# A Strassen-Winograd kernel on one core: two VectorE additions per half unit become one GpSimd addition, with a new GpSimd timetable

## The chip, the cores and the metric

The kernel runs on one core of a Trainium2 chip. The metric is the device time of one launch in microseconds; the median of three runs of the kernel before is 1453.6 us (1452.87 to 1454.05). The profile shown is one further execution of it, with a span of 1452.4 us on that core and a granted TensorE clock of 1.00.

## The reference

A factorization-machine layer over a batch of 1024 rows, 512 features and 64 embeddings of width 512, all in float32. Cut to what matters:

```python
out_lin = x @ lin_w.T + lin_b
xv = einsum('bf,efm->bem', x, weight)                  # x 1024x512, weight 64x512x512
zp = einsum('bf,efm->bem', square(x), square(weight))
return out_lin + 0.5 * sum(square(xv) - zp, axis=1)    # summed over the 64 embeddings
```

Because the second sum is linear in the squared weights, the kernel needs `square(weight)` summed over the embeddings only, and then one product with `square(x)`. The large part is `xv`: 64 products of 1024x512 by 512x512, each squared and added up.

## The kernel before, in words

**Groups and products.** Sixteen groups of four embeddings are worked through (`q` in the main loop, L542). In each, the product of x with the four weights is done by a two-level Strassen scheme in Winograd's form: seven outer products (named "1", "2", "6", "7", "5", "3", "4", in this order, `UNITS` L532), each of them seven inner products. A unit (`unit`, L413) is one outer product for one half `j` of 128 rows; it issues seven TensorE products `p`, each a 128x128 by 128x512 float32 matmul that the trace records as two matmuls, into the PSUM banks x, v and y.

**The timetable.** Every operation is registered with `st.at(t, fn)`, and `Stream.run` (L23) emits them in the order of t. A t orders the instructions in each engine's queue and nothing else: at run time each engine takes its queue in order and waits on semaphores. One group has 98 steps of t, fourteen per outer product, and the 98 products of a group fall on one step each, so a step is the time of one product p. Within a unit that begins at t0 the products stand at t0, +2, +4, ... +12, and the two halves j are seven steps apart and interleave. Work on bank contents is put half a step after the product it follows.

**Engines.** TensorE does the products. ScalarE copies bank x to bank y (L481), squares finished blocks in place (`squares`, L499) and squares weights (`w_squares`, L517). VectorE adds PSUM banks to blocks in SBUF: `to_s`, `join`, `out_of` (L440, L464, L450). GpSimd makes the weight combinations: `outer_t` (L373, 128x1024, two per combined outer operand) and `inner_t` (L384: tp of 128x1024, then t6 and t4 of 128x512, for each outer product). tp is read by TensorE from step 2 of its outer product on, t6 from step 4, t4 from step 12. The tiles tp, t6 and t4 have two buffers each. GpSimd also issues the DMAs that add to memory: `gather` (L509) adds squared blocks to `acc[0]` or `acc[1]` (128x1024, 512 KB each), `w_squares` adds squared weights to `w2_sum` (1 MB each). A gather into a part of `acc` waits for the one before it into the same part to have landed. SyncE loads the weights (`load_w`, L356, four of 1 MB in a group).

**Blocks.** Each group has three result tiles of [2 (u), 2 (j), 2, 512] per partition: "a", "b" and "c" (`place`, L407). "a" and "c" swap places from group to group. Outer product "5" is special (`both`, L417): its four results go to "a" and to "c" both. For the two results that come straight from a bank, `out_of` makes two VectorE additions from PSUM. For the other two, b = 3 and b = 1, `join` leaves the result in the SBUF tile `s`, and from there `rest_a` (L471, VectorE, 128x512, twice per j) adds it into "a" and `rest_dst` (L475, GpSimd, 128x1024, once per j) writes "b" plus it to "c". The next outer product, "3", reads "a" again in `to_s`.

**The end.** After the last group (`g = 98 * NQ`, L612) come `square(x)`, the combinations of it and of `w2_sum` on GpSimd (`last_sx`, `last_tw`), and one more seven-product Winograd step (`last_p`) in two halves s, whose results are joined with `acc`. The last squares of "a" are paired by GpSimd (`pair_up`, L745) and gathered, those of "b" are added to `acc[1]` by VectorE (`add_c21`, L749).

Of the kernel before, what the change touches and what calls it, by code (L numbers as in the profile page):

```python
# [10 lines left out]
ALU = mybir.AluOpType  # L11
# [17 lines left out]
def kernel(  # L29
# [383 lines left out]
    def unit(t0, q, i, j, addend, dst):  # L413


        d = {}
        both = i == "5"  # L417

        def p(o, bank, start):
            def fn():  # L420
                nc.tensor.matmul(  # L421
                    d[bank],
                    xsl(i, o)[:, ts(j, P)],
                    operand_b(q, i, o),
                    start=start,
                    stop=True,
                    skip_group_check=True,
                )

            return fn  # L430

        def p1():
            for n in "xvy":
                d[n] = psum.tile(
                    [P, BK], F32, tag=n, name=f"{n}{q}_{i}{j}", bufs=2 if n == "x" else 3
                )
            d["s"] = spool.tile([P, 2, BK], F32, tag="s", name=f"s{q}_{i}{j}")
            p("1", "x", True)()

        def to_s(bank, b):  # L440
            def fn():
                o = d["s"][:, b // 2]
                if addend is None or both:
                    nc.scalar.copy(o, d[bank])
                else:
                    nc.vector.tensor_add(o, d[bank], zblk(q, addend, j, b))  # L446

            return fn

        def out_of(bank, b):  # L450
            def fn():
                if addend is None:
                    nc.scalar.copy(zblk(q, dst, j, b), d[bank])
                    return
                if both:
                    z = zblk(q, "a", j, b)
                    nc.vector.tensor_add(z, d[bank], z)  # L457
                nc.vector.tensor_add(  # L458
                    zblk(q, dst, j, b), d[bank], zblk(q, addend, j, b)
                )  # L460

            return fn

        def join(bank, b):  # L464
            def fn():
                s = d["s"][:, b // 2]
                nc.vector.tensor_add(s if both else zblk(q, dst, j, b), d[bank], s)  # L467

            return fn

        def rest_a(b):  # L471
            z = zblk(q, "a", j, b)
            nc.vector.tensor_add(z, z, d["s"][:, b // 2])  # L473

        def rest_dst():  # L475
            nc.gpsimd.tensor_add(
                place(q, dst)[:, 1, j], place(q, addend)[:, 1, j], d["s"]
            )

        st.at(t0 + 0, p1)  # L480
        st.at(t0 + 0.5, lambda: nc.scalar.copy(d["y"], d["x"]))  # L481
        st.at(t0 + 2, p("5", "v", True))
        st.at(t0 + 2.5, to_s("v", 3))
        st.at(t0 + 4, p("6", "y", False))
        st.at(t0 + 4.5, to_s("y", 1))
        st.at(t0 + 6, p("2", "x", False))
        st.at(t0 + 6.5, out_of("x", 0))
        st.at(t0 + 8, p("7", "y", False))
        st.at(t0 + 8.5, join("y", 3))
        st.at(t0 + 10, p("3", "v", False))  # L490
        st.at(t0 + 10.5, join("v", 1))
        st.at(t0 + 12, p("4", "y", False))
        st.at(t0 + 12.5, out_of("y", 2))
        if both:
            st.at(t0 + 9.6, lambda: rest_a(3))
            st.at(t0 + 11.6, lambda: rest_a(1))
            st.at(t0 + 12.6, rest_dst)

    def squares(t, q, n, j, wait):  # L499
        z = place(q, n)  # L500
# [6 lines left out]


    def gather(t, q, n, r, j, u):  # L509
        st.at(  # L510
            t,
            lambda: nc.gpsimd.dma_start(  # L512
                acc[r][:, j], place(q, n)[:, u, j], accum_op=ALU.add
            ),
        )

    def w_squares(t, q, v, u):  # L517
        first = q == v == u == 0

        def sq(kk):  # L520
            o = (w2_sum if first else w2_sb)[:, ts(kk, 2)]
            nc.scalar.activation(o, WB[kk][v][:, u], AF.Square)  # L522

        for kk in range(2):
            st.at(t + 0.1 * kk, lambda kk=kk: sq(kk))
        if not first:
            st.at(
                t + 3.5,
                lambda: nc.gpsimd.dma_start(w2_sum, w2_sb, accum_op=ALU.add),
            )  # L530

# [10 lines left out]
    for q in range(NQ):  # L542
        g0 = 98 * q
        last = q == NQ - 1
        for kk, v, t in ((1, 0, -41), (0, 1, -39), (0, 0, -37), (1, 1, -10)):
            if q:
                st.at(g0 + t, lambda q=q, kk=kk, v=v: load_w(q, kk, v))

        for i, t0, t1 in (
            ("5", -13.4, -10.2) if q else ("5", -11, -10.9),  # L550
            ("6", 11, 14.1) if q else ("6", 0.5, 0.6),
            ("7", 24, 24.1),
            ("4", 50, 50.1),
        ):
            for u, t in enumerate((t0, t1)):
                st.at(g0 + t, lambda i=i, u=u: outer_t(i, u))
        for i, *times in (
            ("1", -6.4, -2.9, -2.8) if q else ("1", -11.5, -11.4, -11.3),
            ("2", 3.1, 7.1, 7.2) if q else ("2", -5, -4.9, -4.8),
            ("6", 18.4, 22.1, 22.2),  # L560
            ("7", 31.1, 31.2, 38.1),
            ("5", 43.1, 43.2, 49.1),
            ("3", 57.9, 58, 61.6),
            ("4", 73.1, 80.1, 80.2),
        ):
            for n, t in zip(("tp", "t6", "t4"), times):
                st.at(g0 + t, lambda q=q, i=i, n=n: inner_t(q, i, n))
        for n, (i, (addend, dst)) in enumerate(UNITS.items()):
            for j in range(2):
                unit(g0 + 14 * n + 7 * j, q, i, j, addend, dst)  # L570

        for k, n, r, times in (
            (1, "c", 0, (31, 43, 38, 49)),
            (4, "c", 1, (73, 84.5, 80, 91.5)),
            (5, "a", 0, (87.6, 99, 95, 105)),
            (6, "b", 1, (101, 112, 108.5, 120)),
        ):
            for j in range(2):
                t = g0 + 14 * k + 7 * j + 14.6
                squares(t - (0.95 if last and n == "b" else 0), q, n, j, 3 * (k == 4))  # L580
                if last and n != "c":
                    continue
                for u in range(2):
                    gather(g0 + times[2 * j + u], q, n, r, j, u)
        if q == 0:
            w_times = (-6, 14.8, 36, 54)
        else:
            w_times = (-15, 14.8, 36, 54)
        for n, t in enumerate(w_times):
            w_squares(g0 + t, q, n // 2, n % 2)  # L590
    for kk, v in ((0, 0), (1, 0), (0, 1), (1, 1)):
# [18 lines left out]


    g = 98 * NQ  # L612
    XQ = [WB[0][r].rearrange("p u l (n q) -> p u (l n) q", q=Q) for r in range(2)]
    SX, TW = {}, {}

    def load_xq(r):
# [9 lines left out]
        return SX[i]  # L626

    def last_sx(i):
        t = WB[1][0] if i in "56" else T5
        t = t.rearrange("p u l (n q) -> p u (l n) q", q=Q)  # L630
        SX[i] = t[:, "5673".index(i) % 2]
        a21, a22 = XQ[1][:, 0], XQ[1][:, 1]
# [10 lines left out]
        return w2_sum[:, ts(kk, 2), ts(u, HM)]  # L643

    def last_tw(i):
        t = WB[1][1].rearrange("p u l m -> p (u l m)").rearrange(
            "p (n l c) -> p n l c", l=2, c=HM
        )
        TW[i] = t[:, "5674".index(i)]
# [28 lines left out]
    def last_banks(s):  # L678
        for n in "xvy":
            L[n, s] = psum.tile(  # L680
                [P, BK], F32, tag=n, name=f"{n}_last{s}", bufs=2 if n == "x" else 3
            )

        L["o", s] = place(NQ - 1, "c")[:, s]
        L["t", s] = w2_sb.rearrange("p (r u) c -> p r u c", r=2)

    def blk(n, s, b):
        return L[n, s][:, b // 2, b % 2]
# [52 lines left out]
        )  # L741

    def pair_up(j):  # L745
        z = place(NQ - 1, "a")
        nc.gpsimd.tensor_add(z[:, 0, j], z[:, 0, j], z[:, 1, j])

    def add_c21(j, u):  # L749
        o = acc[1][:, j]  # L750
        nc.vector.tensor_add(o, o, ZT[1][:, u, j])  # L751

    for j in range(2):
        st.at(g - 10.5 + 7 * j, lambda j=j: pair_up(j))
        gather(g - 7.7 + 7 * j, NQ - 1, "a", 0, j, 0)
        for u in range(2):
            st.at(g + (4.6 + 0.1 * u, 8.65)[j], lambda j=j, u=u: add_c21(j, u))

    for r, t in ((1, -39), (0, -37)):
        st.at(g + t, lambda r=r: load_xq(r))  # L760
    for t, r, kk in ((-26, 1, 0), (-25, 1, 1), (-22, 0, 0), (-21, 0, 1)):
        st.at(g + t, lambda r=r, kk=kk: square_xq(r, kk))
    for i, t in zip("5673", (-18, -15, -12, -2)):
        st.at(g + t, lambda i=i: last_sx(i))
    for i, t in zip("5674", (-9, -8, -6, -5)):
        st.at(g + t, lambda i=i: last_tw(i))
    for s, ks in ((0, (0, 3.2, 5.2, 6, 7, 8, 9)), (1, (10, 12, 14, 16, 18, 20, 22))):
        k1, k5, k6, k2, k7, k3, k4 = (g + k for k in ks)
# [19 lines left out]
        else:  # L788
# [5 lines left out]
            for j in range(2):  # L794
                st.at(k4 + j, lambda j=j: end_p(j))
                st.at(k4 + j + 0.5, lambda j=j: end_out(j))
                st.at(k4 + j + 0.6, lambda j=j: store(1, 2, slice(j, j + 1)))
    for t, b in ((11.1, 0), (12.1, 2)):
        st.at(g + t, lambda b=b: last_t(1, b))
    for t, b in ((11.1, 0), (11.2, 1), (11.3, 2), (11.4, 3)):  # L800
        st.at(g + t, lambda b=b: add_acc(0, b))
# [36 lines left out]
```

## Time and profile before

| what | value | where from |
|---|---|---|
| median of three runs | 1453.6 us | the times |
| span of the profiled run | 1452.4 us | the page |
| ScalarE busy | 621.8 us (43%) | the page, part 1 |
| 128x1024 additions on GpSimd, tp from a combined operand, mean as recorded | 3021 ns | groups of instructions, L391 |
| `rest_a` on VectorE | 64 of 1950 ns | groups, L473 |
| `rest_dst` on GpSimd | 32 of 2606 ns | groups, L476 |
| gathers, issue to landing, median | 250 of 7.2 us | DMA issues |
| additions to w2_sum, issue to landing, median | 63 of 9.2 us | DMA issues |
| weight loads, issue to landing, median | 64 of 11.9 us | DMA issues |
| share of the 16 DMA engines, 741 to 828 us | 0.89, at 194 GB/s | busy time by stretch |

How to read it. PE is TensorE's matmuls, DVE VectorE, ACT ScalarE, POOL GpSimd. In a line of the groups, `z<-z,s` names the tile written and the tiles read, and the tail gives the idle time of the engine just before those instructions and what ended it. A line of the waits gives the engine and line that waited, who ended the wait, the sum of the waits in us, how many there were and the longest. Starts and durations in a timeline are us from the span's start. A GpSimd instruction that follows the start of a DMA is recorded from its own dispatch[...]; so costs of GpSimd are read from one end to the next, not from the durations.

### The profile page before, as it was taken

The numbers are of one execution on the slowest core, as the hardware profiler recorded it, in microseconds if no ns is written. First come the engines' busy times: TensorE is split into PE (matmuls) and PEld (weight loads), VectorE is DVE, ScalarE is ACT, GpSimd is POOL, SyncE is SP. The second block draws the span as 40 slices with busy tenths as digits, with TensorE's granted clock in tenths as the row PEclk, the third lists the DMA queues.
The fourth block names the chain that finished last, engine by engine and source line by source line (L and its number), as shares of the span: only waits on it lengthen the run. The fifth ranks groups of instructions, "written<-read, shape, count | busy, mean of one in ns | idle before, by whom it ended". The sixth has DMA issues, their size and how long they took to land.

```text
span 1452.4 us, 11321 instructions
## 1 busy us (share of the span) xinstructions
PE 1411.4 (97%) x3340; PEld 631.5 (43%) x3340; DVE 993.4 (68%) x1341; ACT 621.8 (43%) x824; POOL 1241.6 (85%) x836
## 2 busy tenths in 40 slices
PE   9999999999999999999999999999999999999998
PEld 5444444444444444444444444444444444444446
DVE  6785767857577585766857567585766858567687
ACT  3344353452534444353453534444353453435343
POOL 7778979888897988979888897988979888897984
PEclk9999999999999999999999999999999999999999
DMA  5389898898988889898898988889898898988864
GB/s 210 65 201 213 179 204 173 209 188 204 199 170 212 172 203 210 187 197 169 211 186 202 202 170 212 176 200 212 196 190 165 213 178 206 206 170 212 176 147 115
DMA packets 66749, 272.59 MB, mean 188 GB/s; under 512 B 6400, under 2 KB 8960, under 8 KB 58368
## 3 DMA queue, kind: packets, MB, share of 16 engines
q0 software_dynamic: 45072, 197.15, 69.1%
q1 hardware_dynamic: 21328, 74.19, 16.3%
q10 hardware_dynamic: 288, 0.52, 0.1%
q8 instruction: 27, 0.44, 0.1%
q14 instruction: 34, 0.28, 0.1%
HBM read 72.61 MB, written 2.10 MB: 51 GB/s over the span
## 4 chain that ended last, share of the span: by engine, by line
PE 81%; DVE 9%; issue 5%; POOL 4%; DMA 1%; ACT 0%; DVEq 0%; POOLq 0%
PE y L421 34%; PE x L421 23%; PE v L421 22%; DVE z L473 3%; DVE s L446 1%; PE lin L216 1%; POOL t L393 1%; POOL t L380 1%; DMA acc<-z 1%; DVE s L467 1%; DVE z L458 1%; DVE z L457 1%; DVE z L467 1%; POOL acc L512 1%; DVE acc L751 1%
## 5 line engine op out<-in xcount | busy, mean ns | idle before, releaser
L421 PE MATMUL y<-t,xs 128*128 128x512 f32 x896 | 425.9, 594 | 20.1 <-DVE z L467 19.5
L512 POOL DMA_DIRECT2D acc<-z x250 | 287.8, 1170 | 130.1 <-ACT z L504 70.2
L481 ACT COPY y<-x 128x512 f32<-128x512 f32 x224 | 127.8, 571 | 516.2 <-PE x L421 516.2
L467 DVE TENSOR_TENSOR z<-y,s 128x512 f32<-128x512 f32 x192 | 132.5, 690 | 226.7 <-PE y L421 226.7
L504 ACT ACTIVATE z<-z 128x1024 f32<-128x1024 f32 x256 | 256.8, 1053 | 68.6 <-DVE z L458 68.6
L421 PEld LDWEIGHTS y<-t,xs 128*128 128x128 f32 x896 | 168.2, 190 | 241.5 <-issue 227.6
L421 PE MATMUL x<-w,xs 128*128 128x512 f32 x512 | 248.4, 592 | 0.0
L421 PE MATMUL y<-tp,xs 128*128 128x512 f32 x448 | 230.4, 596 | 15.0 <-DVE s L446 15.0
L421 PE MATMUL v<-tp,xs 128*128 128x512 f32 x448 | 229.0, 593 | 0.0
L391 POOL TENSOR_TENSOR tp<-w 128x1024 f32<-128x1024 f32 x64 | 194.2, 3034 | 0.0
L421 PE MATMUL x<-t,xs 128*128 128x512 f32 x384 | 188.3, 592 | 0.0
L467 DVE TENSOR_TENSOR z<-v,s 128x512 f32<-128x512 f32 x192 | 132.4, 690 | 68.4 <-PE v L421 66.6
L380 POOL TENSOR_TENSOR t<-w,t 128x1024 f32<-128x1024 f32 x64 | 168.3, 2712 | 0.0
L458 DVE TENSOR_TENSOR z<-y,z 128x512 f32<-128x512 f32 x192 | 132.0, 688 | 51.3 <-PE y L421 51.1
L458 DVE TENSOR_TENSOR z<-x,z 128x512 f32<-128x512 f32 x192 | 131.8, 687 | 33.3 <-PE x L421 31.8
L522 ACT ACTIVATE w_sb<-w 128x1024 f32<-128x1024 f32 x126 | 125.8, 1047 | 63.5 <-DMA w_sum<-w_sb 63.5
L421 PEld LDWEIGHTS x<-w,xs 128*128 128x128 f32 x512 | 97.3, 190 | 122.0 <-issue 121.7
L391 POOL TENSOR_TENSOR tp<-t 128x1024 f32<-128x1024 f32 x48 | 145.0, 3021 | 0.0
L421 PEld LDWEIGHTS y<-tp,xs 128*128 128x128 f32 x448 | 83.8, 190 | 127.4 <-issue 98.8
L421 PEld LDWEIGHTS v<-tp,xs 128*128 128x128 f32 x448 | 84.9, 190 | 107.8 <-issue 104.3
L421 PE MATMUL v<-w,xs 128*128 128x512 f32 x256 | 130.7, 592 | 0.0
L446 DVE TENSOR_TENSOR s<-v,z 128x512 f32<-128x512 f32 x160 | 110.3, 689 | 23.8 <-PE v L421 23.3
(115 smaller groups left out, 1569.9 us busy)
## 6 DMA issues: line engine op xcount, KB each, us to landing
acc<-z POOLq DMA_DIRECT2D x250, 512.0 KB, 7.2
w<-weight SPq DMA_DIRECT2D x64, 1024.0 KB, 11.9
w_sum<-w_sb POOLq DMA_DIRECT2D x63, 1024.0 KB, 9.2
w<-x SPq DMA_DIRECT2D x2, 1024.0 KB, 10.1
out<-z SPq DMA_DIRECT2D x7, 256.0 KB, 2.2
xs<-x SPq DMA_DIRECT2D x2, 384.0 KB, 6.8
t<-lin_wT ACTq DMA_DIRECT2D x2, 256.0 KB, 4.3
t<-lin_wT SPq DMA_DIRECT2D x1, 512.0 KB, 6.3
```

The source lines that it names most:

```text
L216: nc.tensor.matmul(LIN[n], quarter(0, kk, (0, 1, 3, 2)[2 * s + l])[:, ts(j, P)], lw_sb[:, 2 * kk + l, :], start=(kk == 0 and l == 0), stop ...
L380: nc.gpsimd.tensor_sub(OUTER[i][:, u], a[:, u], b[:, u])
L391: nc.gpsimd.tensor_sub(t, b[:, 1], b[:, :, 0])
L421: nc.tensor.matmul(d[bank], xsl(i, o)[:, ts(j, P)], operand_b(q, i, o), start=start, stop=True, skip_group_check=True,)
L446: nc.vector.tensor_add(o, d[bank], zblk(q, addend, j, b))
L458: nc.vector.tensor_add(zblk(q, dst, j, b), d[bank], zblk(q, addend, j, b))
L467: nc.vector.tensor_add(s if both else zblk(q, dst, j, b), d[bank], s)
L473: nc.vector.tensor_add(z, z, d["s"][:, b // 2])
L481: st.at(t0 + 0.5, lambda: nc.scalar.copy(d["y"], d["x"]))
L504: lambda u=u: nc.scalar.activation(z[:, u, j], z[:, u, j], AF.Square),
L512: lambda: nc.gpsimd.dma_start(acc[r][:, j], place(q, n)[:, u, j], accum_op=ALU.add),
L522: nc.scalar.activation(o, WB[kk][v][:, u], AF.Square)
```

## The change

For outer product "5", the two `rest_a` additions of VectorE for each j (128x512 each) become one GpSimd addition of 128x1024, next to the one that `rest_dst` makes; VectorE then keeps only additions that read a PSUM bank in the main loop. GpSimd gets this work in place of DMA starts: the gathers of the first "c" and of "b" take both halves j in one DMA of 1 MB instead of two of 512 KB. All t of GpSimd's operations in a group are set anew, and with them those of the weight squares. At the end of the kernel, the pairing of the last "a" squares on GpSimd is dropped: four of the last eight blocks of squares are gathered and four are added by VectorE at later places, the loads of x go to other buffers, and the first combination of the squared x is put between the additions of the last outer product "5".

```diff
-        def rest_a(b):
-            z = zblk(q, "a", j, b)
-            nc.vector.tensor_add(z, z, d["s"][:, b // 2])
-        def rest_dst():
-            nc.gpsimd.tensor_add(
-                place(q, dst)[:, 1, j], place(q, addend)[:, 1, j], d["s"]
-            )
+        def rest(n, src):
+            nc.gpsimd.tensor_add(place(q, n)[:, 1, j], place(q, src)[:, 1, j], d["s"])
...
-            st.at(t0 + 9.6, lambda: rest_a(3))
-            st.at(t0 + 11.6, lambda: rest_a(1))
-            st.at(t0 + 12.6, rest_dst)
+            st.at(t0 + 11, lambda: rest("a", "a"))
+            st.at(t0 + 13.8, lambda: rest(dst, addend))
...
-                t + 3.5,
+                t + 5,
                 lambda: nc.gpsimd.dma_start(w2_sum, w2_sb, accum_op=ALU.add),
...
-            ("5", -13.4, -10.2) if q else ("5", -11, -10.9),
-            ("6", 11, 14.1) if q else ("6", 0.5, 0.6),
-            ("7", 24, 24.1),
-            ("4", 50, 50.1),
+            ("5", -8, 2) if q else ("5", -11, -10.9),
+            ("6", 14.2, 14.3) if q else ("6", 0.5, 0.6),
+            ("7", 28.7, 28.8),
+            ("4", 50, 53),
...
-            ("1", -6.4, -2.9, -2.8) if q else ("1", -11.5, -11.4, -11.3),
-            ("2", 3.1, 7.1, 7.2) if q else ("2", -5, -4.9, -4.8),
-            ("6", 18.4, 22.1, 22.2),
-            ("7", 31.1, 31.2, 38.1),
-            ("5", 43.1, 43.2, 49.1),
-            ("3", 57.9, 58, 61.6),
-            ("4", 73.1, 80.1, 80.2),
+            ("1", -4.3, -0.6, 2.1) if q else ("1", -11.5, -11.4, -11.3),
+            ("2", 6.4, 10.1, 10.2) if q else ("2", -5, -4.9, -4.8),
+            ("6", 20.7, 20.8, 27),
+            ("7", 34.4, 34.5, 39.7),
+            ("5", 43.1, 43.2, 43.3),
+            ("3", 57.9, 58, 61.7),
+            ("4", 81, 81.1, 81.2),
...
-            (1, "c", 0, (31, 43, 38, 49)),
-            (4, "c", 1, (73, 84.5, 80, 91.5)),
-            (5, "a", 0, (87.6, 99, 95, 105)),
-            (6, "b", 1, (101, 112, 108.5, 120)),
+            (1, "c", 0, ((None, 38.8), (None, 52.9))),
+            (4, "c", 1, ((0, 73), (0, 87), (1, 80), (1, 92.8))),
+            (5, "a", 0, ((0, 88), (0, 99.5), (1, 96.5), (1, 107.2))),
+            (6, "b", 1, ((None, 111.3), (None, 124.2))),
...
-    for j in range(2):
-        st.at(g - 10.5 + 7 * j, lambda j=j: pair_up(j))
-        gather(g - 7.7 + 7 * j, NQ - 1, "a", 0, j, 0)
-        for u in range(2):
-            st.at(g + (4.6 + 0.1 * u, 8.65)[j], lambda j=j, u=u: add_c21(j, u))
+    gather(g - 10, NQ - 1, "a", 0, 0, 0)
+    gather(g - 1.5, NQ - 1, "a", 0, 1, 0)
+    gather(g + 1.5, NQ - 1, "a", 0, 0, 1)
+    gather(g + 3.5, NQ - 1, "b", 1, 0, 0)
+    for t, n, r, j, u in (
+        (8.65, "b", 1, 1, 0),
+        (8.7, "b", 1, 1, 1),
+        (8.8, "a", 0, 1, 1),
+        (11.25, "b", 1, 0, 1),
+    ):
+        st.at(g + t, lambda n=n, r=r, j=j, u=u: add_last(n, r, j, u))
...
-    for i, t in zip("5673", (-18, -15, -12, -2)):
+    for i, t in zip("5673", (-24.1, -9.9, -9, -5)):
         st.at(g + t, lambda i=i: last_sx(i))
```

More of the change, by code (lines that the diff above doesn't have):

```diff
@@ L509, in gather, with fn @@
     def gather(t, q, n, r, j, u):
[L510 to L515, printed above, removed]
+        def fn():
+            z = place(q, n)[:, u]
+            o, z = (acc[r], z) if j is None else (acc[r][:, j], z[:, j])
+            nc.gpsimd.dma_start(o, z, accum_op=ALU.add)
+        st.at(t, fn)
     def w_squares(t, q, v, u):
@@ L579 @@
                 t = g0 + 14 * k + 7 * j + 14.6
-                squares(t - (0.95 if last and n == "b" else 0), q, n, j, 3 * (k == 4))
-                if last and n != "c":
-                    continue
-                for u in range(2):
-                    gather(g0 + times[2 * j + u], q, n, r, j, u)
+                squares(t - (0.95 if last and n == "b" else 0), q, n, j, 4 * (k == 4))
+            for m, (j, t) in enumerate(times):
+                if not last or n == "c":
+                    gather(g0 + t, q, n, r, j, m % 2)
         if q == 0:
-            w_times = (-6, 14.8, 36, 54)
+            w_times = (-6, 14.8, 37, 56.6)
         else:
-            w_times = (-15, 14.8, 36, 54)
+            w_times = (-15, 14.8, 37, 56.6)
         for n, t in enumerate(w_times):
@@ L612 @@
     g = 98 * NQ
-    XQ = [WB[0][r].rearrange("p u l (n q) -> p u (l n) q", q=Q) for r in range(2)]
+    XQ = [
+        t.rearrange("p u l (n q) -> p u (l n) q", q=Q) for t in (WB[0][1], WB[1][0])
+    ]
     SX, TW = {}, {}
@@ L628, in last_sx @@
     def last_sx(i):
-        t = WB[1][0] if i in "56" else T5
+        t = WB[0][0] if i in "56" else T5
         t = t.rearrange("p u l (n q) -> p u (l n) q", q=Q)
@@ L645, in last_tw @@
     def last_tw(i):
-        t = WB[1][1].rearrange("p u l m -> p (u l m)").rearrange(
+        t = w2_sb.rearrange("p k m -> p (k m)").rearrange(
             "p (n l c) -> p n l c", l=2, c=HM
@@ L684, in last_banks @@
         L["o", s] = place(NQ - 1, "c")[:, s]
-        L["t", s] = w2_sb.rearrange("p (r u) c -> p r u c", r=2)
+        L["t", s] = T6
     def blk(n, s, b):
@@ L741, in end_out, with add_last @@
         )
[L745 to L751, printed above, removed]
-    for j in range(2):
-        st.at(g - 10.5 + 7 * j, lambda j=j: pair_up(j))
-        gather(g - 7.7 + 7 * j, NQ - 1, "a", 0, j, 0)
-        for u in range(2):
-            st.at(g + (4.6 + 0.1 * u, 8.65)[j], lambda j=j, u=u: add_c21(j, u))
-    for r, t in ((1, -39), (0, -37)):
+    def add_last(n, r, j, u):
+        o = acc[r][:, j]
+        nc.vector.tensor_add(o, o, place(NQ - 1, n)[:, u, j])
+    gather(g - 10, NQ - 1, "a", 0, 0, 0)
[9 more added lines that the diff above has]
+        st.at(g + t, lambda n=n, r=r, j=j, u=u: add_last(n, r, j, u))
+    for r, t in ((1, -40.9), (0, -38.9)):
         st.at(g + t, lambda r=r: load_xq(r))
-    for t, r, kk in ((-26, 1, 0), (-25, 1, 1), (-22, 0, 0), (-21, 0, 1)):
+    for t, r, kk in ((-28, 1, 0), (-27.9, 1, 1), (-25, 0, 0), (-24.9, 0, 1)):
         st.at(g + t, lambda r=r, kk=kk: square_xq(r, kk))
-    for i, t in zip("5673", (-18, -15, -12, -2)):
+    for i, t in zip("5673", (-24.1, -9.9, -9, -5)):
         st.at(g + t, lambda i=i: last_sx(i))
-    for i, t in zip("5674", (-9, -8, -6, -5)):
+    for i, t in zip("5674", (-9.8, -9.7, -8.9, -4.9)):
         st.at(g + t, lambda i=i: last_tw(i))
@@ L797 @@
                 st.at(k4 + j + 0.6, lambda j=j: store(1, 2, slice(j, j + 1)))
-    for t, b in ((11.1, 0), (12.1, 2)):
+    for t, b in ((11.1, 0), (12.6, 2)):
         st.at(g + t, lambda b=b: last_t(1, b))
```

## The prediction, made before the changed kernel was run

> **What bounds the kernel now.** I read part 1 of the page first.
>
> ```profile
> PE 1411.4 (97%) x3340; PEld 631.5 (43%) x3340; DVE 993.4 (68%) x1341; ACT 621.8 (43%) x824; POOL 1241.6 (85%) x836
> ```
>
> TensorE is busy 97% of the span, so all that a change of order can win is its idle 41 us, and in the pipeline's refill after each idle stretch. Next, the waits: who kept TensorE waiting.
>
> ```profile
> PE y L421 <- DVE z L467: 19.5, 17, 1.2
> ...
> PE y L421 <- DVE s L446: 15.0, 16, 1.0
> ...
> PEld y L421 <- POOL t L393: 8.5, 17, 1.0
> ...
> PE y_last L666 <- DVE z L705: 1.6, 1, 1.6
> ```
>
> Two waits for VectorE, 16 times each: once per group. The timeline around one of them:
>
> ```profile
> 702.27 3.33 DVE L473 TENSOR_TENSOR z<-z,s 128x512 f32<-128x512 f32 x1
> ...
> 702.39 2.65 POOL L391 TENSOR_TENSOR tp<-t 128x1024 f32<-128x1024 f32 x1
> ...
> 705.52 0.68 DVE L467 TENSOR_TENSOR s<-v,s 128x512 f32<-128x512 f32 x1
> ...
> 706.12 0.68 DVE L446 TENSOR_TENSOR s<-y,z 128x512 f32<-128x512 f32 x1
> 706.28 2.35 POOL L476 TENSOR_TENSOR z<-z,s 128x1024 f32<-128x1024 f32 x1 [1.24 <-DVE s L467]
> 706.72 2.45 DVE L473 TENSOR_TENSOR z<-z,s 128x512 f32<-128x512 f32 x1
> ...
> 706.85 1.12 PE L421 MATMUL y<-tp,xs 128*128 128x512 f32 x2 [0.94 <-DVE s L446]
> ...
> 711.72 1.10 PE L421 MATMUL y<-t,xs 128*128 128x512 f32 x2 [1.16 <-DVE z L467]
> ```
>
> `rest_a` (L473) takes 3.33 and 2.45 us where GpSimd adds at the same time. VectorE's queue behind it comes late, and TensorE waits for `to_s` (L446) and then for a `join` (L467). The chain of waits shows these additions on the path, and a period:
>
> ```profile
> 706.80 2.10 DVE z L473
> ...
> 793.52 2.10 DVE z L473
> ```
>
> Period 86.72 us. An undisturbed product p takes 0.858 us (four matmul records are 1.72 us in the same chain), so 98 take 84.1: 2.6 us per group are lost. The matmul starts agree: after the four matmuls at the two waits the steps exceed 0.429 us by 1.10, 0.10, 1.33 and 0.07, together 2.60.
>
> GpSimd has the time left. Its costs, from one end to the next:
>
> ```profile
> 753.77 4.68 POOL L380 TENSOR_TENSOR w<-w,w 128x1024 f32<-128x1024 f32 x2
> 758.38 0.87 POOL L512 DMA_DIRECT2D acc<-z  x1
> 758.99 2.66 POOL L391 TENSOR_TENSOR tp<-w 128x1024 f32<-128x1024 f32 x1
> 761.73 1.27 POOL L393 TENSOR_TENSOR t<-w,tp 128x512 f32<-128x512 f32 x1
> 762.94 0.87 POOL L512 DMA_DIRECT2D acc<-z  x1
> 763.55 1.57 POOL L395 TENSOR_TENSOR t<-w,t 128x512 f32<-128x512 f32 x1
> ```
>
> The ends are 758.45, 759.25, 761.65, 763.00, 763.81, 765.12. So a 128x1024 addition costs 2.36 us (4.68 for two, 2.40 for the third), a 128x512 one 1.33, a DMA start 0.81; starts of 1 MB additions to w2_sum show the same 0.83.
>
> **What the Trainium skill says.** "SBUF — State Buffer", section "Who interferes with whom": a VectorE operation with two SBUF inputs shares a read interface with a GpSimd operation that reads SBUF, exclusively, and one fully blocks the other; with one SBUF input it doesn't. The trace agrees: L473 takes 0.69 to 3.33 us, additions with a PSUM input 0.67 to 0.69 whatever GpSimd does. "GPSIMD Engine Reference", section 3.1: a float32 `tensor_tensor` of 2048 elements takes 4497 ns on GpSimd; half of it is an estimate of 2.25 us for 1024, and the trace's 2.36 is what I use. "DMA: Bandwidth & Descriptors", section "Anatomy of one DMA": a DMA's semaphore wait is made by the issuing sequencer, so a gather that waits holds up all of GpSimd's queue; the trace has such waits of up to 3.8 us ("POOL acc L512 <- DMA acc<-z"). The same page, "Queues, rings and completion order": the DMA engines alternate between queues, so weight loads and additions share them; the trace shows landings of 4.6 us alone and 11 to 14 us in the crowded stretch.
>
> **The change part by part.**
>
> *VectorE.* 64 operations of 1950 ns leave its queue, 125 us. None of what remains in the main loop, but for eight short bias additions, has two SBUF inputs. In the tightest eight steps (6.9 us) around "5" and "3", eleven PSUM additions remain; back to back they take 0.60 each, 6.6 us, and each is released at least two steps before TensorE needs it. Both waits go: 16 x 2.6 = 41.7 us.
>
> *GpSimd's sum.* Before, per group: 17 additions of 128x1024, 14 of 128x512, 20 DMA starts: 17 x 2.36 + 14 x 1.33 + 20 x 0.82 = 75.1 us of 86.7. After: 19, 14 and 16: 44.8 + 18.6 + 13.1 = 76.6 of 84.1. 7.5 us are left for its waits.
>
> *GpSimd's timetable*, in steps (additions 2.75 and 1.55, DMA starts 0.95), where it must wait or is awaited:
> - The join before `rest("a")` of j = 0 ends about step 68.1. 70.9 `rest("a")`, 73.6 `rest("c")`, 74.6 gather. j = 1 is released at 75.1: 77.9, 80.6, gather 81.6. `to_s` of "3" reads "a" at 73 and 80: two steps (1.8 us) to spare each.
> - Queued behind are the operands of "4": tp 84.4 (due 86), t6 85.9 (due 88), t4 87.5 (due 96). 1.6 steps, 1.4 us, to spare; the narrowest place.
> - Then gathers and the next group: 88.4, 89.4, w2_sum 90.4, outer "5" 93.1, gather 94.1, tp "1" 96.8 (due 100), gather 97.8, t6 99.3 (due 102), gather 100.3, outer "5" 103, t4 104.6 (due 110), tp "2" 107.3 (due 114). The next gather waits for the one at 97.8 to land. Ahead of it are 3 MiB of additions and most of a 1 MB load from 87.5 on. In the trace 4 MiB took from step 86 to 111.2, 0.16 MiB a step; so it lands at about 111 to 112. Then t6 "2" ends at 114.5 (due 116), t4 116, gather 117, outer "6" 122.5, w2_sum 123.5, tp "6" 126.2 (due 128).
> - From there the queue gains: outer "7" ends at 136 (due 140), tp "7" 138.6 (due 142), tp "5" 146.3 (due 156), the fourth outer operand at 154 to 156, tp "3" 158.7 (due 170), t4 162.8. `rest("a")` is released at 166.1: 3.3 steps of rest. The period of 98 steps closes.
>
> *Five groups* have extra waits of TensorE for t6 or tp (periods of 87.1 to 87.4 in the chain): 2.4 us in all. The due times above leave 1.5 steps where these had none; I take them as gone, too.
>
> *DMA.* The merged gathers move the same bytes. In the trace's packet records a 4 KB addition packet takes 337 ns, an 8 KB one 639, so 35 ns are saved per pair. Per group the engines need 8 x 2.70 + 8 x 5.11 + 4 x 3.36 = 75.9 us of 84.1: share 0.90 as now. It costs nothing. "c" is overwritten at step 71 and its second gather, issued at 54 to 55, lands by 67 with the 9.2 us that 1 MB additions take.
>
> *The weight squares* move 2.6 steps later at 56.6; ScalarE then waits less for w2_sum (63.5 us in the waits now), off the path.
>
> *The end.* Two `add_c21` additions (9.5 us, blocked by GpSimd) stand ahead of the `minus_half` that TensorE waits 1.63 us for; after, they stand behind it: 1.9 us gone with the refill. They lie behind GpSimd's last work, where the trace shows 1.25 us each, so they end before the second half needs `acc`. Against this, in the last group a 128x1024 combination is put between the two j of `rest`: `rest("a")` of j = 1 ends at 80.1, tp of "4" at 86.5 instead of 86: 0.7 us lost.
>
> Sum: 41.7 + 2.4 + 1.9 - 0.7 = 45.3; 1453.6 - 45.3 = 1408.3. For GpSimd lateness of the kind that five groups show, I leave 0.7: 1409.
>
> **The rivals.**
> - *GpSimd takes VectorE's place as the one awaited*, at tp "4" or after the crowded gathers. For it: 1.4 us to spare, landings that vary by 2 us (11.2 to 14.1). Against: all other places have more, and eleven groups in sixteen lost nothing to GpSimd before. With 1 us per group: 1409 + 16 = 1425.
> - *VectorE still late.* Eleven additions in eight steps leave 0.3 us. If half the loss stays: 1409 + 21 = 1430.
> - *GpSimd becomes the bound.* If its waits of now (10.4 us in one group: 4.3 for squares, 3.6 for landings, 2.5 for VectorE) stay and the shorter period adds 1 us to the landings, the period is 76.6 + 10.4 + 1 = 88.0 against 86.9 on average now: 1453.6 + 16 x 1.1 - 1.2 = 1470, slower. Without the extra, no change. Against it: the waits now come partly from `rest_a` itself (3.1 us for a square behind it), and waits that lie inside the slack shrink by themselves.
>
> **How the numbers follow.** Forecast 0.73; GpSimd awaited 0.15; VectorE late 0.05; GpSimd the bound 0.05; no change 0.02. Low end: all waits gone and none new is 1453.6 - 46.0 = 1407.6; I take 1405 for unsure starts. High end: the first rival, 1426. That leaves out about 0.12. Faster 0.93, same 0.02, slower 0.05.
>
> **What would show it.** Right: waits of TensorE for `to_s` and `join` near zero; periods of 84.1 us; GpSimd's rows of `rest` near 2.36 us; GpSimd idle before `rest("a")`; DMA share about 0.90. Wrong: TensorE waiting for tp or t6 of "4", "2" or "6" in each group, or GpSimd's idle time before gathers above 7.5 us per group.

## The result, and the profile after

The changed kernel takes 1413.39 us (median of four runs, 1413.10 to 1414.48) against 1453.57 us before: a ratio of 0.9725, interval 0.9708 to 0.9742, or 40.2 us less. 1409 had been forecast, with 1405 to 1426 as the range. The profiled execution has a span of 1411.2 us, 41.2 less than the one before.

Part 1 of the page of the changed kernel:

```profile
PE 1402.8 (99%) x3340; PEld 633.7 (45%) x3340; DVE 883.1 (63%) x1277; ACT 623.2 (44%) x824; POOL 1244.5 (88%) x806
```

VectorE's busy time fell by 110 us. GpSimd's stayed where it was (1241.6 before), because 60 DMA starts paid for 32 more additions; of the shorter span it is 88% instead of 85%. TensorE is busy 99%.

The waits of the changed kernel, with who waited, for whom, the sum in us, the number and the longest:

```profile
POOL z L472 <- DVE s L467: 46.3, 31, 3.0
...
POOL acc L506 <- DMA acc<-z: 33.2, 20, 4.4
...
ACT w_sb L515 <- DMA w<-weight: 23.5, 12, 3.3
...
PEld y L421 <- POOL t L393: 4.8, 8, 1.3
...
PEld y L421 <- DVE s L446: 4.0, 4, 1.0
...
DVE acc L348 <- DMA acc<-z: 3.1, 4, 1.5
...
PE y L421 <- DVE z L467: 1.8, 1, 1.8
```

The 34.5 us in which TensorE waited for `to_s` (L446) and `join` (L467) are gone: of the second one wait is left, at the start of the program, and of the first a few short ones, in groups 1 to 4. In their place stand waits that were not there: ScalarE for weight loads (L515; the same line was L522 and waited for w2_sum), VectorE at the bias additions (L348) for a gather.

GpSimd's queue around outer product "5" in the changed kernel, to be laid beside the timeline of before:

```profile
763.96 4.68 POOL L472 TENSOR_TENSOR z<-z,s 128x1024 f32<-128x1024 f32 x2 [2.69 <-DVE s L467]
768.59 0.85 POOL L506 DMA_DIRECT2D acc<-z  x1
769.98 4.67 POOL L472 TENSOR_TENSOR z<-z,s 128x1024 f32<-128x1024 f32 x2 [0.55 <-DVE s L467]
774.60 0.86 POOL L506 DMA_DIRECT2D acc<-z  x1
775.21 2.65 POOL L391 TENSOR_TENSOR tp<-t 128x1024 f32<-128x1024 f32 x1
```

Two additions take 4.68 us, 2.34 each, undisturbed. GpSimd rests 2.69 us before the first pair. In steps of the timetable, counted from the group's own products, these starts are 68.2, 73.6, 75.2, 80.6 and 81.3, and tp of "4" ends at 84.4: the working had 68.1, 73.6, 75.1, 80.6 and 84.4. The pair two groups later starts at 932.19, so a period is 84.1 us.

VectorE in the same stretch, the sequence in which two additions of 3.33 and 2.45 us stood before:

```profile
767.41 0.69 DVE L467 TENSOR_TENSOR s<-y,s 128x512 f32<-128x512 f32 x1
768.34 0.69 DVE L446 TENSOR_TENSOR s<-v,z 128x512 f32<-128x512 f32 x1 [0.24 <-PE v L421]
769.20 0.69 DVE L467 TENSOR_TENSOR s<-v,s 128x512 f32<-128x512 f32 x1 [0.17 <-PE v L421]
769.99 0.69 DVE L446 TENSOR_TENSOR s<-y,z 128x512 f32<-128x512 f32 x1
```

VectorE now waits for TensorE, not the other way round. Every one of these additions, which read a PSUM bank, takes 0.69 us, and all but the third overlap with one of GpSimd's.

**What is left of TensorE's waits.** From the matmul starts after the start of the program, by what exceeds 0.429 us at a wait and at the slower step after it: 1.71 us for `to_s` in groups 1 to 4; 1.30 us for ScalarE's copy y <- x in three groups and 0.19 for a copy to s in one; 1.71 us for t6 of outer product "2" in three groups; 0.63 us for tp of "4" in the last group. Together 5.5 us, where the working had 1.4 (0.7 for the last group, 0.7 in reserve). That is the 4 us between forecast and result. One of each, from the timelines of the changed kernel. First GpSimd, with the gather that waits:

```profile
1049.47 2.66 POOL L391 TENSOR_TENSOR tp<-w 128x1024 f32<-128x1024 f32 x1
1056.50 0.88 POOL L506 DMA_DIRECT2D acc<-z  x1 [4.38 <-DMA acc<-z]
1057.11 1.58 POOL L393 TENSOR_TENSOR t<-w,tp 128x512 f32<-128x512 f32 x1
```

Then TensorE at this place:

```profile
1058.75 1.55 PE L421 MATMUL y<-t,xs 128*128 128x512 f32 x3 [0.19 <-POOL t L393]
```

The gather of "a" starts at step 15.8, and t6 behind it (L393) ends at 18.4, where it was due at 18. Second, ScalarE at the weight squares and TensorE behind it:

```profile
694.12 2.00 ACT L515 ACTIVATE w_sb<-w 128x1024 f32<-128x1024 f32 x2 [3.30 <-DMA w<-weight]
696.03 0.58 ACT L475 COPY y<-x 128x512 f32<-128x512 f32 x1
```

```profile
696.75 1.53 PE L421 MATMUL y<-t,xs 128*128 128x512 f32 x3 [0.58 <-ACT y L475]
```

Third, VectorE at a bias addition: it waits for the merged gather of "b", then lasts longer than 0.69 us as GpSimd adds beside it, and `to_s` behind it comes late:

```profile
148.06 1.24 DVE L348 SCALAR_TENSOR_TENSOR acc<-bias,acc 128x512 f32<-128x512 f32 x1 [1.54 <-DMA acc<-z]
```

### The profile page after: what moved, and what is told of

It is laid out like the page before. It is cut to its first block, busy times and chain, and to the rows that moved or that the text cites. A ratio compares the mean times of both kernels' runs of the same rounds, so it can differ in the third digit from the quotient of the medians.

```text
span 1411.2 us, 11148 instructions
## 1 busy us (share of the span) xinstructions
PE 1402.8 (99%) x3340; PEld 633.7 (45%) x3340; DVE 883.1 (63%) x1277; ACT 623.2 (44%) x824; POOL 1244.5 (88%) x806
## 4 chain that ended last, share of the span: by engine, by line
PE 80%; POOL 9%; DMA 8%; issue 2%; DVE 1%; ACT 0%; POOLq 0%; ACTq 0%; DVEq 0%
PE y L421 33%; PE v L421 22%; PE x L421 21%; DMA acc<-z 5%; DMA w<-weight 3%; POOL t L380 2%; POOL tp L391 2%; POOL z L472 1%; POOL t L393 1%; PE lin L216 1%; POOL acc L506 1%; POOL t L395 1%; PE y_last L660 1%; POOL w_sum L522 1%; PE x_last L660 0%
## 5 line engine op out<-in xcount | busy, mean ns | idle before, releaser
L467 DVE TENSOR_TENSOR z<-y,s 128x512 f32<-128x512 f32 x192 | 132.8, 692 | 237.1 <-PE y L421 236.0
L497 ACT ACTIVATE z<-z 128x1024 f32<-128x1024 f32 x256 | 260.2, 1054 | 22.7 <-POOL z L472 20.2
L506 POOL DMA_DIRECT2D acc<-z x190 | 196.4, 1056 | 68.9 <-DMA acc<-z 33.2
L472 POOL TENSOR_TENSOR z<-z,s 128x1024 f32<-128x1024 f32 x64 | 149.9, 2364 | 46.3 <-DVE s L467 46.3
L391 POOL TENSOR_TENSOR tp<-w 128x1024 f32<-128x1024 f32 x64 | 175.5, 2743 | 4.1 <-PE y L421 2.9
L467 DVE TENSOR_TENSOR z<-v,s 128x512 f32<-128x512 f32 x192 | 132.7, 691 | 71.0 <-PE v L421 69.2
L380 POOL TENSOR_TENSOR t<-w,t 128x1024 f32<-128x1024 f32 x64 | 159.3, 2567 | 0.0
L515 ACT ACTIVATE w_sb<-w 128x1024 f32<-128x1024 f32 x126 | 126.0, 1050 | 28.0 <-DMA w<-weight 23.5
L391 POOL TENSOR_TENSOR tp<-t 128x1024 f32<-128x1024 f32 x48 | 137.1, 2855 | 0.0
```

Source lines behind the costliest of these rows:

```text
L380: nc.gpsimd.tensor_sub(OUTER[i][:, u], a[:, u], b[:, u])
L391: nc.gpsimd.tensor_sub(t, b[:, 1], b[:, :, 0])
L472: nc.gpsimd.tensor_add(place(q, n)[:, 1, j], place(q, src)[:, 1, j], d["s"])
L497: lambda u=u: nc.scalar.activation(z[:, u, j], z[:, u, j], AF.Square),
L506: nc.gpsimd.dma_start(o, z, accum_op=ALU.add)
```

## The experiments

The theory to test is that VectorE's additions with two SBUF inputs were late because GpSimd's additions block them, and that the move takes this away. The rivals are that VectorE had too many operations there, and that the new timetable, not the move, brought the gain. Then the 5.5 us that are left are looked for. All times are medians; the kernel before took 1452.7 to 1453.5 us beside them.

### The move alone

```diff
 # kernel before
...
-            st.at(t0 + 9.6, lambda: rest_a(3))
-            st.at(t0 + 11.6, lambda: rest_a(1))
-            st.at(t0 + 12.6, rest_dst)
+            st.at(t0 + 11, lambda: rest("a", "a"))
+            st.at(t0 + 12.6, lambda: rest(dst, addend))
```

> The kernel before with one edit: VectorE's two additions per half become one GpSimd addition at t0 + 11; the old timetable, the old gathers of 512 KB and the old end stay. If the gain comes from taking these additions off VectorE, TensorE's waits for to_s and join of outer product 5 (34.5 us) nearly vanish. GpSimd's sum is then 75.1 + 2 x 2.36 = 79.8 us per group; with some 5 us of waits that it can't avoid, the period is about 84.8 us, and the rest of the loss turns up as TensorE waiting for tp, t6 and t4: 1415 to 1432, about 1423. If the timetable were the cause of the gain, it stays above 1445.

1417.31 us, ratio 0.9752 (0.9739 to 0.9766): the move alone is enough for 36 of the 40 us. In the waits of this kernel TensorE waits for GpSimd instead, though not long:

```profile
PEld y L421 <- POOL t L393: 21.4, 34, 1.0
```

By the matmul starts that is about 0.3 us per group, for t6 of outer product "6" above all; the old end of the kernel adds 2.5 us of waits (0.67 and 1.79 us by the matmul starts).

### The timetable without the move

The two additions go back to VectorE; the new timetable, the merged gathers and the changed end stay.

```diff
 # kernel after
...
-            st.at(t0 + 11, lambda: rest("a", "a"))
+            st.at(t0 + 9.6, lambda: rest_a(3))
+            st.at(t0 + 11.6, lambda: rest_a(1))
```

> The changed kernel with one edit: the two additions of each half go back to VectorE at t0 + 9.6 and t0 + 11.6; timetable, merged gathers and end stay as changed. If the move is what brings the gain, TensorE waits again for VectorE in each group: 1430 to 1455. If the timetable alone does it (GpSimd has no addition of operands between the two halves any more, so fewer of VectorE's additions meet one), the waits are under 0.5 us per group and it takes 1413 to 1421. The additions themselves should fall from a mean of 1950 ns before towards 690 ns where they meet no GpSimd addition.

1428.42 us, ratio 0.9829 (0.9815 to 0.9842): 25 us less than before, and a miss on both sides, since neither expectation named the middle. The time without the move is 15 us above the kernel with both. The additions left on VectorE, by their line in the trace of this kernel (minimum, median and maximum in ns):

```profile
L473 DVE TENSOR_TENSOR z<-z,s x64: 681/692/3340, 87.0 to 1376.6; 128x512 f32<-128x512 f32 x64
```

and before:

```profile
L473 DVE TENSOR_TENSOR z<-z,s x64: 691/2125/3358, 86.9 to 1401.4; 128x512 f32<-128x512 f32 x64
```

The new timetable has no operand made between GpSimd's two additions, so most of VectorE's no longer meet one: 18 of 64 take over 1 us instead of 43. By the matmul starts the loss behind outer product "5" is left in the last group alone, with 2.6 us. The 15 us stand elsewhere: t6 of "2" comes late in thirteen groups (8.5 us, at the place shown above, against 1.7), and in groups 1 to 4 `to_s` comes late behind the bias additions (6.0 us, against 1.7). Why these two places are worse here was not tried. So move and timetable are two ways to take away the same loss and don't add up: 36, 25, and 40 together.

### tp of outer product 4 out of the way

```diff
 # kernel before
-            ("4", 73.1, 80.1, 80.2),
+            ("4", 80.05, 80.1, 80.2),
```

> The kernel before with one edit: GpSimd makes tp of outer product 4 after its second addition for outer product 5, not between the two, so that it has nothing to do while the first of VectorE's late additions runs. All of VectorE's operations stay. If the meeting with GpSimd is the cause, the additions of 3.33 us fall to about 0.7, VectorE is 2.6 us earlier, the first wait of TensorE (1.2 us with the refill) vanishes and the second, behind the addition that still meets one of GpSimd's, shrinks: 1420 to 1435. If VectorE's number of operations is the cause, it stays above 1450.

1437.32 us, ratio 0.9896 (0.9880 to 0.9913). With all 64 additions still on VectorE, 1.7 us are left of TensorE's 34.5 us of waits for VectorE, at the start of the program. The addition that was blocked at this place takes 0.68 us, the next one, which meets `rest_dst`, still 2.47. But GpSimd is no earlier within the group than before. The gather ahead of tp of "4" waits 3.1 us for a square, as it did in the kernel before, and its queue stays late: in fifteen groups TensorE waits for tp of the next outer product, "1", by 1.1 us at the matmul starts, in the last group for tp of "4":

```profile
PE v L421 <- POOL tp L391: 15.6, 16, 2.0
```

That VectorE's waits vanish was as expected; the time, just above the range, includes waits for GpSimd that I had not counted.

### Number of operations or blocking

Two further VectorE additions per half on top of the changed kernel, which leave the results as they are:

```diff
 # kernel after
+        def dummy(n):
+            a = d["v"] if FROM_PSUM else d["s"][:, 1 - n]
+            nc.vector.tensor_add(d["v"], a, d["s"][:, n])
...
+            for n in range(2):
+                st.at(t0 + 11.6, lambda n=n: dummy(n))
```

With one PSUM and one SBUF input:

> The changed kernel with two further VectorE additions per half in outer product 5, of one PSUM and one SBUF input, into the spent PSUM bank v, at the place of the ones removed (t0 + 11.6); their results are not used. It puts back the number of VectorE's operations, not the meeting with GpSimd. If the number was what made VectorE late, most of the loss comes back: 1440 to 1455. If it was the blocking by GpSimd's additions, fifteen additions of 0.6 to 0.7 us in eight steps are 9.0 to 10 us in 6.9, late by some 2.5 us of which 1.7 us are slack: up to 0.8 us per group, 1414 to 1426.

With two SBUF inputs:

> The same two further additions, but with both inputs in the SBUF tile s and the output in the same PSUM bank; their results are not used. They are released together with the GpSimd addition of the same half, so each meets GpSimd's work. If the blocking is the cause, they take 1 to 3 us each instead of 0.6 to 0.7 and the loss comes back: 1435 to 1465, and more than the run with PSUM inputs by at least 15 us. If the number is the cause, both runs take the same.

1414.88 us (0.9735, 0.9721 to 0.9748) and 1502.18 us (1.0344, 1.0329 to 1.0360). The two groups, as busy time, mean ns and idle time before; first the PSUM form:

```profile
L473 DVE TENSOR_TENSOR v<-v,s 128x512 f32<-128x512 f32 x64 | 44.6, 697 | 1.6
```

then the SBUF form:

```profile
L473 DVE TENSOR_TENSOR v<-s 128x512 f32<-128x512 f32 x64 | 139.4, 2179 | 1.6
```

The same number of additions at the same place costs 1.5 us over the changed kernel in one form, which is within the spread of its own runs (1412.61 to 1416.12), and 89 us in the other. That shows the cause: not the number, but the meeting with GpSimd. Some 18 of the 89 us are matmuls that ran at half the granted clock behind the long waits (last section). The second form does worse than the kernel before, since for the second half both additions fall in with a pair of GpSimd's that stand back to back: each is held up by one of the two, and the pair of VectorE's takes 5.21 us.

```profile
817.88 5.21 DVE L473 TENSOR_TENSOR v<-s 128x512 f32<-128x512 f32 x2
```

### What is left: the bias additions

```diff
 # kernel after
-        for r, t in enumerate((22.6, 36.6)):
+        for r, t in enumerate((22.6, 45.6)):
```

> The changed kernel with one edit: the four bias additions to acc[1] stand at 45.6 instead of 36.6. In the trace after, VectorE waits at them up to 1.5 us for the merged gather of b to land, in groups 1 to 4, and TensorE then waits 0.32 to 0.47 us for to_s: 1.7 us in all. If that is so, these four waits vanish and the time falls by 1.7 us, to about 1411.7. If the waits came from VectorE's own load, they stay.

1413.77 us (0.9730, 0.9717 to 0.9743): nothing won. The wait for the gather is gone, but at the new place the addition meets a GpSimd addition (up to 2.2 us), and in two of the four groups TensorE still waits for `to_s`, by 0.3 to 0.4 us each. The bias addition has two SBUF inputs, too.

### What is left: the weight squares

```diff
 # kernel after
-            w_times = (-15, 14.8, 37, 56.6)
+            w_times = (-13.2, 14.8, 37, 56.6)
```

> The changed kernel with one edit: the first pair of weight squares stands at -13.2 instead of -15, behind the copy of unit 4, j = 0 and the squares of a. In the trace after, ScalarE waits 23.5 us for weight loads at these squares, and in three groups the copy behind them comes late for TensorE (0.82, 0.33 and 0.15 us). If that is the mechanism, ScalarE's wait for the load falls below 6 us and the time by about 1.3 us, to 1412; the gathers of a behind these squares start one step earlier as well, which can win up to 1 us more where GpSimd is late afterwards.

1412.65 us (1412.48 to 1412.69), ratio 0.9719 (0.9706 to 0.9732): 0.7 us less, half of what was expected, and too little to tell from the changed kernel by the ratios (0.9725, 0.9708 to 0.9742). ScalarE no longer waits for the load, and TensorE no longer for the copy. The waits at the bias additions grew instead, from 1.71 to 3.0 us by the matmul starts.

### What is left: the gather ahead of t6

```diff
 # kernel after
-            (5, "a", 0, ((0, 88), (0, 99.5), (1, 96.5), (1, 107.2))),
+            (5, "a", 0, ((0, 88), (0, 99.5), (1, 96.5), (1, 108.9))),
```

> The changed kernel with one edit: the gather of a (j = 1, u = 1) stands at 108.9 instead of 107.2, behind t6 and t4 of outer product 2 instead of ahead of them. In the trace after, it waits up to 4.4 us for the gather before it into the same part of acc to land, and in three groups t6 behind it ends at step 18 when it is due at 18: 0.46, 0.74 and 0.51 us of TensorE with the refill. If that is the mechanism, these three waits vanish and the time falls by 1.7 us, to about 1411.7, and TensorE's waits for GpSimd t (L393) fall below 3 us. If GpSimd were late for want of time, the lateness moves on to tp of outer product 6, and nothing is won.

1408.40 us (1408.20 to 1408.61), ratio 0.9692 (0.9679 to 0.9705): 5.0 us less than the changed kernel, three times the expectation. The three waits for t6 are gone, and with them those for the bias and for ScalarE's copy; by the matmul starts only the 0.6 us in the last group stay. GpSimd in the trace of this kernel, at the place shown above:

```profile
1048.14 1.28 POOL L393 TENSOR_TENSOR t<-w,tp 128x512 f32<-128x512 f32 x1
1049.49 1.27 POOL L395 TENSOR_TENSOR t<-w,t 128x512 f32<-128x512 f32 x1
1052.22 1.77 POOL L506 DMA_DIRECT2D acc<-z  x2 [1.46 <-ACT z L453]
1053.37 5.32 POOL L380 TENSOR_TENSOR t<-w,t 128x1024 f32<-128x1024 f32 x2
```

t6 and t4 are made in the time in which GpSimd had waited, and its queue is about four steps earlier from there on: only the first gather of "b" stands between this gather and outer product "6", and no longer t6 and t4. So the second gather of "b", on which the bias additions wait, and all behind it come earlier. ScalarE's wait for weight loads falls from 23.5 to 1.0 us. The three kinds of wait had one source.

### All four edits

The weight squares and the gather as above, the bias additions at 64.6, where GpSimd rests, and `last_sx("5")` at -16.5 instead of -24.1.

> The changed kernel with four edits: the weight squares at -13.2 and the gather behind t6, as in the runs before it; the bias additions to acc[1] at 64.6, where GpSimd has nothing to do (in the run with 45.6 they met GpSimd's additions and took up to 2.2 us); the first combination of the squared x behind the operands of outer product 4. If the 5.1 us of small waits in the trace after have these four causes, it takes 1413.4 - 1.7 - 1.3 - 1.7 - 0.6 = 1408.1. If others take their place, it stays above 1411.

1408.05 us (1407.81 to 1409.55), ratio 0.9691 (0.9678 to 0.9705). The wait in the last group is gone, but its 0.6 us can't be told from the spread: this kernel and the one with the gather alone are the same by measurement. They are the fastest that were run.

### What the merged gathers are for

```diff
 # kernel with the gather behind t6
-            (1, "c", 0, ((None, 38.8), (None, 52.9))),
+            (1, "c", 0, ((0, 38.8), (0, 52.9), (1, 38.9), (1, 53))),
-            (6, "b", 1, ((None, 111.3), (None, 124.2))),
+            (6, "b", 1, ((0, 111.3), (0, 124.2), (1, 111.4), (1, 124.3))),
```

> The changed kernel with the gather behind t6 (1408.4 us), and the merged gathers of 1 MB taken apart again: four DMAs of 512 KB for the first c and four for b. GpSimd's sum rises by 4 x 0.82 = 3.3 us per group, from 76.6 to 79.9 us of 84.1; its rest before the additions of outer product 5 (2.7 us, plus 0.5) is used up. If these starts were what had to go to make room, TensorE waits for GpSimd by 0.3 to 1 us per group: 1413 to 1425. If GpSimd has the room anyway, it takes under 1410. The run with the old timetable and the move alone (1417.3 us), where TensorE waited for t6 and tp by some 0.3 us per group, speaks for about 1414.

1413.14 us (0.9726, 0.9711 to 0.9740): 4.7 us more than with the merged ones. GpSimd's rest before `rest` falls from 51.3 to 34.2 us in the whole run, but TensorE doesn't wait for GpSimd's operands. It waits as in the changed kernel: for `to_s` behind the bias additions in groups 1 to 4 (3.3 us) and for ScalarE's copy behind the weight loads in two groups (1.6 us). So the merging makes room, and the lateness shows on other engines first. The time is at the lower edge of what was expected, but the wait that it was expected from, TensorE's for GpSimd, did not come. Whether the further starts or the smaller transfers make these engines late was not separated.

## Why the prediction was right, and where it was off

**The loss per group: right.** 2.6 us in each of sixteen groups were read from the chain's period and from the matmul starts; the period of an undisturbed group is 84.1 us now, and no wait behind outer product "5" is left. That blocking was the cause is shown by the pair of runs with further additions (1414.9 and 1502.2 us).

**VectorE still late: rightly given little.** Four further additions per group from PSUM cost no more than 1.5 us in the whole run.

**GpSimd's timetable: right in the stretch around "5", to 0.1 step.** The costs taken from end to end (2.36, 1.33, 0.82 us) held: a pair of `rest` takes 4.68 us.

**The step that was off: the landing after the crowded gathers.** It was put at step 111 to 112 (13 to 14 of the next group), from a rate of 0.16 MiB a step. The gather behind it waited 2.7 to 4.4 us in each of fifteen groups (where the list of waits names ScalarE for it, the landing is meant: the copy named writes another tile). It started at 13.8 to 15.0 in the twelve groups that lost nothing, and at 15.8 to 16.1 in the three that lost time; t6 then ended at 18.4 to 18.7 and not at 114.5, that is 16.5. Its narrow margin had been named as the first rival, at 1 us per group; it came to 1.7 us in all. The term was mis-sized by about two steps in these groups.

**What was missed: who else is behind that gather.** I looked only at the weight squares that were moved, called them "off the path", and passed over the first pair of the next group, whose place (-15) did not change; and I did not follow the gather of "b" to the bias additions. The first pair waits up to 3.3 us for a weight load, and cost 1.3 us through ScalarE's queue (the copy y <- x stands behind the squares); the bias additions cost 1.7 us through VectorE's. One moved gather took all of it away, so these are one fault: GpSimd's queue, late by about four steps, makes the transfers behind it late.

**The five groups: gone, but with a successor.** Their 2.4 us, for t6 of "6", are gone as forecast; 1.7 us of the like turned up at t6 of "2". With these, the parts add up: 41.7, 2.4 and 1.9 won, and 5.5 us of waits that are left in their place, give 40.5; 40.2 were measured.

**The end: right.** TensorE's wait of 1.63 us for VectorE is gone; the wait in the last group, forecast as 0.7 us, is 0.63 us, and moving the first combination of the squared x takes it away.

**DMA: right.** A share of 0.89 from 741 to 828 us, as before, at 196 GB/s.

**GpSimd as the bound: did not come.** Its waits ahead of gathers fell from 130 to 69 us in the whole run, 4.3 us per group, in the direction that was argued.

## What to carry to other kernels

Where two engines block each other, first look for the few operations of the one that have the blocking form: here 64 of 1341 of VectorE's made the whole difference, and as many more in another form cost almost nothing. Moving the operation away and moving the other engine's work out of its way took away the same loss here; they are worth trying one at a time before both. In a queue that also starts DMAs, put work that is ready and soon due ahead of a start that has to wait for a landing, and when checking a margin follow not only the next instruction but every engine that waits for a DMA behind it.

## What the runs showed of the hardware that was not expected

**A blocked addition can miss its turn.** In the run with two further SBUF additions, 47 of the 64 were held up. Of these 46 took 2.5 to 2.7 us: each waited for one GpSimd addition and got in behind it, even where GpSimd's next one stood ready. One, in the last group, took 6.30 us, the first of the two in this line of VectorE:

```profile
1444.34 7.03 DVE L473 TENSOR_TENSOR v<-s 128x512 f32<-128x512 f32 x2
```

GpSimd beside it:

```profile
1442.82 2.66 POOL L635 TENSOR_TENSOR w<-w 128x1024 f32<-128x1024 f32 x1
1445.15 4.92 POOL L476 TENSOR_TENSOR z<-z,s 128x1024 f32<-128x1024 f32 x2
```

It waited for the rest of one GpSimd addition and for two whole ones. The kernel before has another case: the first of the `add_c21` additions, 1.23 us undisturbed, took 8.14 us while GpSimd worked through four. In the traces of all the kernels here there are 115 places where one GpSimd addition ends and the next begins while a VectorE addition of this form waits. At 104 of them VectorE got in; there the next is recorded as starting less than 0.1 us before the end of the one ahead, if at all. At 11 it did not, in four VectorE additions at the ends of four kernels; there the overlap is 0.25 us or more. Whether the overlap decides was not tried.

**Blocking goes both ways.** Where VectorE's addition started first, GpSimd's took 2.87 us (at 697.35 us of the kernel before) instead of 2.35.

**A clock at half behind some waits.** In the same run the granted clock over the run was 0.986. It fell to half for 3.41 us, twice for 6.83, behind ten of the sixteen waits of 3.1 us or more for outer product "5", and the next three to six matmuls started about 0.85 us apart instead of 0.43. The trace tells the ten from the others: the falls lie on a grid of 3.413 us. Where TensorE was idle for 2.02 to 3.35 us within one stretch of this grid, the next stretch ran at half; where the wait was spread over two stretches, with at most 1.89 us in either, it did not. The single wait of 3.0 us in the run with PSUM inputs, which no slow matmuls followed, is of the second kind: counted on such a grid back from the end of that run, it has 1.6 and 1.5 us in two stretches. This is read from one trace; no run was made to try it.
